# VectorE's order in the front of a conditioned residual kernel: products taken out of their bank first in a period, sums and rotary factors last

## The chip, the core and the metric

The kernel is written for Trainium2 and runs on one core of one chip. A core has TensorE (PE: matmuls, and its weight loads, PEld), VectorE (DVE), ScalarE (ACT), GpSimd (POOL) and SyncE (SP), which here only issues DMAs. Each engine works off its own list of instructions in order and waits on semaphores for the others. TensorE writes its results into PSUM[...]; VectorE and ScalarE read them from there.

The metric is the device time of one execution in microseconds (us), the median over several runs.

## The reference

`x` has 64 batches of 32 rows and 512 columns, in float32. Four layers are added to it one after the other:

```python
x = x + _L0_cond_ref(x, itok_B_0_15, L0_cond_weights)        # x mixed over its 32 rows by one of 16 matrices
x = x + _L1_cond_ref(x, itok_B_6_15, base_weight, base_bias, lora_A_w, lora_B_w)
x = x + _L2_cond_ref(x, Wq, Wk, Wv, Wo, q_norm_w, k_norm_w, k_cache, v_cache, table, seqlens)
x = x + _L3_cond_ref(x, L3_cond_weights, itok_B_0_15)        # mixed over its rows again
```

- Layers 0 and 3: `einsum('bct,bcd->bdt', x, W)`, with the 32 x 32 matrix `W = weights[condition]`.
- Layer 1: `x @ base_weight.T + base_bias`, plus a LoRA term of rank 16, `(x @ A.T) @ B.T`, whose A and B are picked for each batch out of 32 adapters.
- Layer 2: attention. q (32 heads of 128), k and v (8 heads of 128) are projections of x. q and k are normalised by their root mean square, weighted and turned by rotary angles of the position. Keys and values are 512 cached rows (16 pages of 32 rows, picked by a table, masked by the cache's length) and the 32 new ones. Softmax, the weighted sum of values, and an output projection `Wo` from 4096 to 512 columns follow.

## The kernel before

**Tiling.** The 64 x 32 rows of x are 16 tiles `t` of 128 rows (4 batches each). The 8 heads of k and v are two groups `g` of 4 (`KG`), with 16 heads of q each. A `Unit` is one batch in one group, 128 of them; it takes 4 periods, one for each head of k.

**Periods.** All of layers 0 to 2 is one list of numbered periods. The function `slot(i)` (L1193) writes out the instructions of period `i`, which fixes each engine's order. What has to happen in which period is entered beforehand by `at(slot, where, do, ...)` into lists by name ("pe", "late", "power", "turn", "dve", "keep", "act", "store", ...), and `run(slot, where)` (L940) emits one list in the order in which its entries were made. The whole runs under a manual schedule, so nothing is moved afterwards. Periods from 0 on hold the attention: scores of one head, softmax, transposes of its result two periods later, and products with the values three periods later.

**The front.** Periods -43 to -1 come before the first scores. In them run

- layers 0 and 1, class `First`, one tile in two periods. In the even period TensorE multiplies by LoRA's A (`h_ps`, L474), by three of four parts of the base weight (`l_ps`, L490), mixes the next tile (`mix_ps`, L435) and transposes an earlier result (`x2T_ps`, L452); VectorE masks the ranks (`hT`, L484) and adds the mix to x (L444). In the odd period TensorE does the rest of `l_ps` and transposes the next tile (`x1T_ps`); VectorE adds the product to x (L444) and lays out a later tile's mixing matrix (`mix_diag`, L426). GpSimd adds the bias (L447) and issues the gathers;
- the transposes of 16 blocks of cached keys, class `Turn` (`page_rows`, L272), which SyncE loads (L256) and stores again (`kT`, L293; values L289). There are 5 buffers for the loaded rows, so a load waits for the store of the block five before it;
- the rotary factors of all 16 tiles, `rotary` (L382): four VectorE instructions for a tile, or eight or twelve in a period, whose results SyncE stores (L397);
- the projections of the first pair of tiles.

**Projections.** Two tiles form a pair, and for k and v together and for each two heads of q a `Block` computes them with seven products in place of eight. It needs sums of blocks of weights (`block_sum`, L615, one instruction of 128 x 1024) and of the transposed x (`First.sums`, L516 to L520, four instructions), both made by VectorE. Each product is two chunks of two matmuls (`project`, L651), in one or two periods as the table in the plan has it. A product's PSUM tile is `proj_ps`, in a pool with one buffer; some products between periods -11 and -3 lie in `s_ps` instead. `take` reads a finished product out and adds it to what it belongs to (`raw`, L663): on ScalarE for the first product of a block, on VectorE for the six others (two instructions for the sixth). The next product can't begin in the bank before. Afterwards a head's squares go to ScalarE (L707), the power to GpSimd (L714), and four pieces (scale L719, straight L726, swapped L738, sum L748) to VectorE, which `norm_piece` (L950) deals out, up to three in a period; then TensorE transposes the heads (`head_ps`, L756).

**VectorE's order in a period.** "late" and "power" hold the work of layers 0 and 1, then comes one piece of a norm, and after it the list "dve", then two more pieces. The list "dve" was begun when the plan was set up: the rotary factors, the weights' sums and the sums of x are in it from then on. The takes are put into it by `begin_block` (L973), when a block begins, and so stand behind these.

**Into the attention.** In period -7 SyncE loads the next pair's `x_12` over the one that TensorE reads last in that period; in period -6 it issues the 16 page loads of the first unit's keys (`kT`, L794), which the first scores wait for.

**After the attention** the output projection (`out_ps`, L1320) and layer 3 (`mix_ps`, L1338) run, from about 2096 us on.

Of the kernel before, what the change touches and what calls it, by code (L numbers as in the profile page):

```python
# [77 lines left out]
def resid_kernel(  # L78
# [149 lines left out]
    with ExitStack() as l2:  # L228
# [708 lines left out]
        def at(slot, where, do, *args):  # L937
            plan.setdefault((slot, where), []).append((do, args))

        def run(slot, where):  # L940
            for do, args in plan.pop((slot, where), ()):
                do(*args)
# [7 lines left out]
        def norm_piece(slot):  # L950


            if not pieces or pieces[0][0] > slot or busy.get(slot, 0) >= 2 + (slot % 4 == 1):
                return
            busy[slot] = busy.get(slot, 0) + 1
            _, piece, norm = pieces.pop(0)
            piece()
            if norm:
                slot += 1
                while slot in turning or (slot - VLAG) % KG == KG - 1:  # L960
                    slot += 1
                turning.add(slot)
                at(slot, "turn", norm.turn)
                at(slot, "keep", norm.keep)
# [8 lines left out]
        def begin_block(pair, b, slots):  # L973
            block = Block(pair, b, slots)
            for i in range(7):
                for c in (0, 1):
                    at(slots[2 * i + c], "pe", block.project, i, c)
                last = slots[2 * i + 1]
                norm = None
                if i in (1, 4, 5, 6):  # L980
                    if b != KV:
                        norm = Norm(pair, i // 5, 2 * b + (i in (4, 5)))
                    else:
                        norm = Norm(pair, i // 5)
                    if b == KV and i in (1, 6):
                        at(last, "store", block.store_values, norm, i // 5)
                    else:
                        at(last, "pe", begin_norm, last, norm)
                at(last, "act" if i == 0 else "dve", block.take, i, norm)
                busy[last] = busy.get(last, 0) + (0, 1, 1, 1, 1, 2, 1)[i]  # L990

        def call(table, key, name, *args):
# [9 lines left out]
        for i in range(n_pairs):  # L1002
# [14 lines left out]
            for b, slots in (  # L1017
                (KV, (0, 0, 1, 2, 3, 3, 4, 5, 6, 6, 7, 8, 9, 9)),
                (0, (10, 11, 12, 12, 13, 14, 15, 15, 16, 17, 18, 18, 19, 20)),
                (1, (21, 21, 22, 23, 24, 24, 25, 26, 27, 27, 28, 29, 30, 30)),  # L1020
            ):
                slots = [home + w for w in slots]
                at(slots[0], "fetch", begin_block, i, b, slots)
# [169 lines left out]
        def slot(i):  # L1193
            run(i, "fetch")
            run(i, "pool")
            new, k = None, i % KG
            if 0 <= i < n:
                new = unit_of[i // KG]
                new.scores(k)
            if LAG <= i < n + LAG:  # L1200
                turned = unit_of[(i - LAG) // KG]
                turned.flip((i - LAG) % KG)
            run(i, "pe")
            run(i, "late")
            run(i, "power")
            norm_piece(i)
            if LAG <= i < n + LAG and (i - LAG) % KG == KG - 1:
                turned.flip_new()
            run(i, "turn")
            if i >= VLAG:  # L1210
                old = unit_of[(i - VLAG) // KG]
                old.values((i - VLAG) % KG)
                if (i - VLAG) % KG == KG - 1:
                    old.values_new()
                    at(i, "act", old.finish)
                    if old.j == NB - 1:
                        at(i + 1, "store", old.store)
            if new:
                new.divide(k)
            run(i, "dve")  # L1220
            norm_piece(i)
            norm_piece(i)
            run(i, "keep")
            run(i, "act")
            run(i, "store")
# [270 lines left out]
```

## Time and profile before

| | |
|---|---|
| Runs | 2500.81, 2500.87, 2497.43 us; median 2500.81 |
| Profiled execution | 2498.24 us; span from first to last instruction 2496.5 us |
| Busy over the span | PE 98%, PEld 74%, DVE 64%, ACT 56%, POOL 47% |
| Mean granted clock of TensorE | 0.997 |
| First product of the projections (period -33) | 43.3 us |
| First scores (period 0) | 218.5 us |
| First product of the output projection after the attention | 2112.4 us |

How to read the views: the stages' view gives for each stretch the busy time of each engine, the granted clock of TensorE as a share of full speed, and DMA. The view of waits names who waited for whom, with the total, the number of waits and the longest. The timeline lists instructions by start and duration; in brackets at the end stands the idle time of the engine before it, with the releaser that the profile infers from semaphores. "issue" there means that it shows none. Instructions overlap in the engine's pipeline, so the distance from start to start is shorter than the duration. In the DVE timeline the line L663 is `take`, L615 a weight sum, L382 rotary factors, L516 to L520 sums of x, L444 an addition to x.

### The profile page before, as it was taken

What the parts mean: (1) busy time and instruction counts of PE and PEld (TensorE: products, weight loads), DVE (VectorE), ACT (ScalarE), POOL (GpSimd) and SP (SyncE); (2) the same over time, 40 slices, a digit from 0 to 9 for tenths busy, and PEclk for the clock granted to TensorE, in tenths of its full rate; (3) what the DMA queues carried; (4) which work ended last, traced back from release to release, by engine and by line L of the source; (5) the groups of instructions that cost most, each with busy time, mean ns of one, the idle gap of its engine ahead of it and who ended that gap; (6) DMA issues with size and microseconds to landing.
All of it is one profiled execution on the core that took longest, in us unless ns stands there. A gap on an engine that the chain in (4) does not pass through costs nothing.

```text
span 2496.5 us, 47363 instructions
## 1 busy us (share of the span) xinstructions
PE 2445.1 (98%) x13760; PEld 1857.8 (74%) x13760; DVE 1609.0 (64%) x3602; ACT 1398.9 (56%) x4135; POOL 1163.0 (47%) x1096
## 2 busy tenths in 40 slices
PE   7799999999999999999999999999999999999999
PEld 4455777777777777777777777777777788888887
DVE  5657777767777677777776777777777766433222
ACT  2225777777767676767777777777777765000000
POOL 4335655555555555655555555655555663000000
PEclk9999999999999999999999999999999999999999
DMA  7775666666666667766565656666657784333221
GB/s 244 237 218 182 190 196 192 203 184 201 184 201 185 200 193 239 242 188 194 178 199 173 188 176 189 176 186 176 193 169 220 247 267 149 115 128 127 86 85 60
DMA packets 448546, 459.19 MB, mean 184 GB/s; under 512 B 51425, under 2 KB 379489, under 8 KB 440481
## 3 DMA queue, kind: packets, MB, share of 16 engines
q1 hardware_dynamic: 398384, 291.24, 38.0%
q0 software_dynamic: 49904, 164.93, 21.6%
q8 instruction: 112, 1.84, 0.3%
q14 instruction: 146, 1.19, 0.2%
HBM read 384.66 MB, written 79.69 MB: 186 GB/s over the span
## 4 chain that ended last, share of the span: by engine, by line
PE 92%; DMA 2%; DVE 2%; issue 2%; SPq 1%; POOL 1%; ACT 0%; DVEq 0%; POOLq 0%; ACTq 0%
PE proj_ps L651 22%; PE o_ps L893 17%; PE out_ps L1320 15%; PE s_ps L838 10%; PE s_ps L841 8%; PE pT_ps L880 8%; PE head_ps L756 3%; PE l_ps L490 2%; PE o_ps L905 2%; DMA kT<-kT 1%; DMA v_sb<-v,v_rows 1%; SPq L794 1%; PE s_ps L873 1%; PE h_ps L474 1%; PE mix_ps L1338 1%
## 5 line engine op out<-in xcount | busy, mean ns | idle before, releaser
L105 POOL DMA_INDIRECT v_sb<-v,v_rows x512 | 539.2, 1053 | 362.3 <-PE o_ps L893 252.9
L846 DVE CUSTOM_DVE_ANT_0 sm<-s_ps,pen 128x544 f32<-128x544 f32 x512 | 370.9, 724 | 462.4 <-PE s_ps L841 449.9
L893 PEld LDWEIGHTS o_ps<-pT,v_sb 128*128 128x128 f32 x4096 | 518.8, 192 | 133.6 <-issue 124.8
L857 ACT ACTIVATE sm<-sm,top 128x544 f32<-128x544 f32 x512 | 382.0, 746 | 342.8 <-DVE top L846 342.7
L893 PE MATMUL o_ps<-pT,v_sb 128*128 128x128 f32 x4096 | 541.2, 275 | 2.4 <-DMA v_sb<-v,v_rows 2.4
L863 ACT ACTIVATE sm<-sm,share 128x512 f32<-128x512 f32 x512 | 369.9, 722 | 170.3 <-DVE share L862 169.0
L882 DVE COPY pT<-pT_ps 128x512 f32<-128x512 f32 x512 | 351.1, 686 | 1.9 <-PE pT_ps L880 1.9
L838 PE MATMUL s_ps<-kT,qT 128*128 128x288 f32 x1024 | 347.0, 420 | 4.5 <-DMA kT<-kT 3.8
L880 PE MATMUL pT_ps<-ident,sm 128*128 128x128 f32 x2048 | 307.3, 273 | 0.0
L841 PE MATMUL s_ps<-kT,qT 128*128 128x256 f32 x1024 | 305.0, 380 | 1.9 <-issue 1.5
L880 PEld LDWEIGHTS pT_ps<-ident,sm 128*128 128x128 f32 x2048 | 255.8, 141 | 51.3
L809 POOL TENSOR_SCALAR pen<-key_f,seq_f 128x544 f32<-128x544 f32 x128 | 279.3, 2182 | 11.8 <-DMA kT<-kT 0.5
L712 POOL TENSOR_SCALAR ss<-ss 128x4 f32<-128x4 f32 x160 | 54.1, 338 | 448.0 <-ACT sq L707 447.6
L841 PEld LDWEIGHTS s_ps<-kT,qT 128*128 128x128 f32 x1024 | 194.2, 190 | 56.9 <-issue 3.4
L663 DVE TENSOR_TENSOR raw<-proj_ps,raw 128x512 f32<-128x512 f32 x332 | 223.5, 685 | 9.7 <-PE proj_ps L651 4.4
L707 ACT ACTIVATE sq<-raw 128x128 f32<-128x128 f32 x640 | 197.1, 308 | 29.7 <-DVE raw L663 14.5
L651 PE MATMUL proj_ps<-sum,x 128*128 128x512 f32 x380 | 189.7, 602 | 8.0 <-DVE raw L663 7.9
L1370 ACT COPY p<-out_ps 128x256 f32<-128x256 f32 x7 | 2.6, 372 | 333.1 <-PE out_ps L1320 333.1
L714 POOL TENSOR_TENSOR rstd<-ss,minus_half 128x4 f32<-128x4 f32 x160 | 183.0, 1144 | 13.3
L105 POOL DMA_INDIRECT mix_rows<-in_w,cond_rows x32 | 32.7, 1021 | 309.8 <-DVE mix_diag L171 300.0
L838 PEld LDWEIGHTS s_ps<-kT,qT 128*128 128x128 f32 x1024 | 154.7, 191 | 21.9 <-issue 4.8
L1320 PE MATMUL out_ps<-w,o_in 128*128 128x256 f32 x768 | 167.1, 379 | 0.0
(175 smaller groups left out, 3499.4 us busy)
## 6 DMA issues: line engine op xcount, KB each, us to landing
kT<-kT SPq DMA_DIRECT2D x2048, 64.0 KB
o<-oT SPq DMA_DIRECT2D x29, 1024.0 KB
o_in<-o SPq DMA_DIRECT2D x28, 1024.0 KB
page_rows<-in_kv_cache SPq DMA_DIRECT2D x32, 256.0 KB
v<-in_kv_cache SPq DMA_DIRECT2D x32, 256.0 KB
kT<-page_rows SPq DMA_DIRECT2D x32, 256.0 KB
vn<-raw SPq DMA_DIRECT2D x32, 256.0 KB
v_sb<-v,v_rows POOLq DMA_INDIRECT x512
```

The costliest lines, as they stand in the source:

```text
L105: nc.gpsimd.indirect_dma_start(out=dst, out_offset=None, in_=table, in_offset=bass.IndirectOffsetOnAxis(ap=index, axis=0),)
L651: nc.tensor.matmul(self.ps, lhsT=self.pair.x[x][:, c if x == "b" else half.start + c, :], rhs=blocks(self.b)[w][:, c, :], start=(c == 0), ...
L809: nc.gpsimd.tensor_scalar(self.pen, key_f, seq_f[:, self.b : self.b + 1], BIG, ALU.is_ge, ALU.mult)
L838: nc.tensor.matmul(ps[:, first:HID], lhsT=q, rhs=self.kT[:, :n1, k, :], start=True, stop=True)
L841: nc.tensor.matmul(ps[:, HID : first + LA], lhsT=q, rhs=self.kT[:, n1:, k, :], start=True, stop=True)
L846: nc.vector.tensor_tensor_reduce(out=sm, in0=ps[:, first : first + LA], in1=self.pen, scale=1.0, scalar=3e38, op0=ALU.add, op1=ALU.min, ac ...
L857: nc.scalar.activation(sm, sm, AF.Exp, bias=top, scale=-1.0, accum_out=total)
L863: nc.scalar.activation(sm[:, :L], sm[:, :L], AF.Copy, scale=share)
L880: nc.tensor.transpose(ps[:, c, :], self.sm[k][:, c * P : (c + 1) * P], ident)
L882: nc.vector.tensor_copy(pT, ps)
L893: nc.tensor.matmul(self.o_ps[k], lhsT=self.v[c][:, k * D : (k + 1) * D], rhs=self.pT[k][:, c, :], start=(c == 0), stop=False,)
L1320: nc.tensor.matmul(ps[:, :HALF], lhsT=o[:, i, :], rhs=w[i // REP][:, i % REP, :], start=(i == 0), stop=(i == KG * REP - 1),)
```

## The change

In the front (periods below 0) VectorE's takes get a list of their own, "take", which `slot` runs directly behind the list "pe", ahead of layers 0 and 1's work of the period. What is left in the list "dve" there, the sums of weights and of x and the rotary factors, is run at the end of VectorE's work in the period, behind all three pieces of norms. From period 0 on nothing is changed: the takes are in "dve" and it is run where it was.

```diff
@@ begin_block
                     else:
                         at(last, "pe", begin_norm, last, norm)
-                at(last, "act" if i == 0 else "dve", block.take, i, norm)
+                at(last, "act" if i == 0 else "take" if last < 0 else "dve", block.take, i, norm)
                 busy[last] = busy.get(last, 0) + (0, 1, 1, 1, 1, 2, 1)[i]
@@ slot
             run(i, "pe")
+            run(i, "take")
             run(i, "late")
             run(i, "power")
             norm_piece(i)
...
             if new:
                 new.divide(k)
-            run(i, "dve")
+            if i >= 0:
+                run(i, "dve")
             norm_piece(i)
             norm_piece(i)
+            run(i, "dve")
             run(i, "keep")
             run(i, "act")
             run(i, "store")
```

## The prediction

> **What bounds the kernel now.** I read TensorE's busy time by stage first. Columns: stretch, length, busy us (and count) of PE, PEld, DVE, ACT, POOL, granted TensorE clock, DMA share, GB/s.
>
> ```profile
> 0.00:43.30 43.30, 30.02 (x107) 17.77 (x108) 20.30 (x39) 8.37 (x13) 20.28 (x33) 1.00 0.80 261
> 43.30:205.50 162.20, 140.62 (x525) 77.45 (x524) 96.92 (x218) 41.05 (x110) 53.76 (x53) 0.95 0.67 213
> 205.50:231.10 25.60, 20.31 (x82) 11.65 (x80) 21.23 (x47) 16.90 (x50) 18.12 (x19) 1.00 0.69 203
> 231.10:2096.00 1864.90, 1858.42 (x11207) 1408.50 (x11208) 1333.96 (x3108) 1321.09 (x3935) 1054.37 (x970) 1.00 0.66 198
> 2096.00:2496.50 400.50, 395.70 (x1848) 342.40 (x1846) 136.54 (x193) 11.48 (x30) 16.44 (x22) 1.00 0.27 99
> ```
>
> From 231 us on TensorE idles 11.3 us in 2265. The front from the first product (43.3, period -33) to the end of period -7 (205.5) idles 21.6 us of 162.2, at clock 0.95. DMA share 0.67 and DVE 60% say that neither is full there. The waits of PE in that stretch name the releaser (total, times, longest):
>
> ```profile
> PE proj_ps L651 <- DVE raw L663: 15.3, 8, 4.1
> PE proj_ps L651 <- issue: 5.1, 1, 5.1
> PE proj_ps L651 <- ACT raw L671: 1.2, 1, 1.2
> ```
>
> So it is the products' single bank (`proj_ps`): the next product waits until `take` has read the last. The timeline around the longest wait, PE then DVE, shows that the 5.1 filed under "issue" is the same thing:
>
> ```profile
> 87.47 1.02 PE L651 MATMUL proj_ps<-wk,x 128*128 128x512 f32 x2
> 88.33 0.60 PE L452 MATMUL x1T_ps<-ident,x_sb 128*128 128x128 f32 x4
> 94.00 3.65 PE L651 MATMUL proj_ps<-sum,x_b 128*128 128x512 f32 x4 [5.08 <-issue]
> ```
> ```profile
> 86.12 1.22 DVE L615 TENSOR_TENSOR sum<-wq,wq 128x1024 f32<-128x1024 f32 x1
> ...
> 88.87 0.69 DVE L444 TENSOR_TENSOR x_sb<-l_ps,x_sb 128x512 f32<-128x512 f32 x1
> 89.47 0.96 DVE L426 TENSOR_TENSOR mix_diag<-mix_rows,same 128x128 f32<-128x128 f32 x1
> 90.35 0.41 DVE L516 TENSOR_TENSOR x<-x_b 128x256 f32<-128x256 f32 x1
> ...
> 92.62 1.28 DVE L663 TENSOR_TENSOR raw<-proj_ps,raw 128x512 f32<-128x512 f32 x2
> 98.58 0.29 DVE L484 TENSOR_TENSOR hT<-h_ps,lora_mask 128x128 f32<-128x128 f32 x1 [4.68 <-PE h_ps L474]
> ```
>
> The product is complete at 88.3, yet VectorE does a weight sum, 8 factors, the addition, sums of x and 4 factors before the takes at 92.62; then it idles 4.68 us. Work is in the wrong order, not too much of it. And the product after the wait runs 3.65 us instead of 1.88.
>
> [...]waits of 2.77, 3.16, 4.09 and 5.08 us were followed by half rate, 2.39 us (at 218.47) was not. [...]the takes start only after all that stands ahead. [...]here mix_diag took 0.96 us at 89.47, against 0.29 elsewhere, beside GpSimd's bias addition at 89.02. I keep 1 us a tile for it.
>
> **The change, part by part.** No instruction is added or removed: 3361 rows on VectorE in both; TensorE, ScalarE, GpSimd and SyncE keep their order. Only VectorE's order in periods below 0 changes.
>
> (a) Takes go first. What it can free: 15.3 + 5.1 = 20.4 us of waits, plus the half clock: 3.65, 3.63 and 3.62 against 1.88 at 94.00, 138.50 and 175.78 (5.3 us), and at 122.97 until the next mix product 6.98 against 4.33 us in the undisturbed period at 107.92 (2.65 us). Together 7.9, so at most 28.3 us. The 1.2 us behind ScalarE's take stay.
>
> (b) Sums and factors go last, so they now stand ahead of the *next* period's take. I laid both orders side by side at the issue intervals of the DVE timeline: take and addition 0.60, weight sum 1.13, factor 0.20, four sums of x 1.46, swapped 0.67, scale or rotary sum 0.60, hT and diag 0.20. In an even period the tail starts when the mix product ends: 0.1 + addition 0.6 + sums and factors. TensorE meanwhile does x2T 0.44, the rest of l_ps 1.72, its product 0.86 or 1.72, transposes 0.44 each. The worst is -26 to -25: tail 0.7 + 1.13 + 8 x 0.20 = 3.44 us; two takes end at 4.64; TensorE wants the bank at 0.44 + 1.72 + 0.86 + 0.44 = 3.46. **Wait 1.2 us** where it was 5.08. For -28 the tail is 2.96 against 3.88 at which the product ends; for -22, 3.5 against 4.3; for -20, 2.6 against 3.5; behind the double take of -15 TensorE waits 0.1. After odd periods the take has slack: the longest tail (12 factors in -27) ends 3.8 us after its product, and hT, queued behind it, is needed at 7.8. So 1.3 us stay[...].
>
> (c) Behind a take that waits for its product stand the addition, diag and hT. The addition is wanted by x2T one period later, behind product, h_ps, l_ps and mix (0.86 + 0.89 + 2.58 + 0.87 = 5.2 us); it comes at most 1.5 us later. Nothing.
>
> (d) Behind the factors stand SyncE's stores of them (28 `rot` stores), and behind these the loads of x and pages. They come up to 2 us later in the period. Page loads run 17.6 us (154.01 to the transpose at 171.6) or more ahead of use; that lead hides it. Without it each would cost its 2 us.
>
> (e) After period -7 the chain is SyncE's, not VectorE's: the load of x_12 waits for TensorE's last read, then 16 page DMAs are issued.
>
> ```profile
> 205.55 0.32 SPq L586 DMA_DIRECT2D x<-xS  x1
> 206.74 10.04 SPq L794 DMA_DIRECT2D kT<-kT  x16
> ```
>
> The first scores start at 218.47, 13 us after 205.5. The take wait of 1.67 us at 213.66 shrinks to about 0.6 and becomes wait for kT: 2.39 grows to about 3.5 us, gain nothing, and the clock now halves there. Price: between 0 (hidden behind the v_sb wait that ends at 231.04) and 1.8 us; I take 0.7.
>
> Sum: 28.3 - 1.3 - 1.3 - 0.7 = 25.0 us. The profiled execution took 2498.24 us (span 2496.5 and 1.7 around it), 2.6 below the median of 2500.81. Profile after: about 2473; median: **2475.5 us** (-1.0%). From 231 us on all moves earlier unchanged: VectorE's order for periods 0 and up is the same.
>
> **Rivals.**
> R1, the page loop becomes the bound: in the front each page's load waits for the store of the page five before. 149.58 (store) to 154.01 (load) is 4.4 us, the loop 6.0 us (147.99 to 154.01). Periods -23 to -12 cost TensorE 70.1 us, less 10.2 waits and 4.4 half clock: 55.5 / 11 = 5.05 us each. So SyncE falls behind 0.95 us a period. Against it: lead 17.6, less 3 periods x 1.3, less 5 x 0.95, leaves about 9 us where a load needs some 4.4. For it: the same bytes in 16% less time, share 0.67 to 0.79. If landing grows to 7 us, five loops lose 2.6 us each, 13 us in all: 2489.
>
> R2, the waits only move to the tails: each even tail 1.5 us longer than laid out[...] returns about 1.5 to 3 us in four or five periods and, past 2.8 us, the half clock: 10 us lost, 2486.
>
> R3, slower: R1 with the loop at full price. Each us of landing costs 5 us over five loops once the lead is gone; the gain of 25 is eaten and the end passes 2501 only when landing exceeds about 10.5 us against 4.4, so 2508 at 12. Only DMA engines full for long could do that; 343 and more GB/s was moved around 15 us at share 0.93, the front needs 255.
>
> R4, no effect: excluded by order unless DVE's order weren't what holds the bank; the timeline says it is. 2500.
>
> **How the numbers follow.** Main case 0.70 (own range 2469 to 2482: the ceiling of 28.3 us taken from the fastest run, 2497.43, up to 6 us less gain than forecast); R1 0.11, R2 0.12, R3 0.04, R4 0.03. The range 2469 to 2488 holds the main case, R2 and part of R1. Faster than 0.2% (below 2495.8, about what a measurement can tell from no change): 0.70 + 0.12 + 0.10 = 0.92; same 0.04; slower 0.04.
>
> **What would show it.** Right: the waits of `proj_ps` for `raw` between the first product and the first scores fall from 20.4 us to under 4, no piece of that stretch but the first scores at half clock, the stage of 162.2 us near 137, kT's wait before the first scores longer than 2.39. Wrong: PE waiting for page_rows or x_sb from DMA (R1), DVE idle in L382 on DMA stores of `rot` and new waits of 2 to 3 us at takes of odd periods (R2), or a changed length of the stretch after the first scores.

## The result, and the profile after

| | before | after |
|---|---|---|
| Runs, us | 2497.43 to 2501.68, median 2500.84 (4) | 2471.99 to 2476.62, median 2472.82 (4) |
| Ratio after / before | | 0.9893, 95% interval 0.9876 to 0.9911 |
| Span of the profiled execution | 2496.5 us | 2471.8 us |
| First product / first scores | 43.27 / 218.47 us | 44.22 / 191.17 us |

The kernel is 28.0 us faster by the medians (1.1%), 24.7 us by the two profiled spans. The forecast was 25.3 us by the median (2500.81 to 2475.5), 2.7 us less than measured; its range held the result.

The first view is again TensorE's busy time by stage, of the kernel after, cut at the same events (start, first product, end of the last product of period -7, the wait of the first products with the values, `o_ps`); the last cut lies 1864.9 us behind that in both kernels. Columns: stretch, length, busy us (and count) of PE, PEld, DVE, ACT, POOL, granted TensorE clock, DMA share, GB/s.

```profile
0.00:44.20 44.20, 30.61 (x106) 17.95 (x107) 20.26 (x39) 8.34 (x13) 20.32 (x33) 1.00 0.77 255
44.20:178.30 134.10, 131.39 (x524) 74.18 (x523) 94.97 (x216) 40.60 (x110) 57.15 (x53) 1.00 0.79 258
178.30:205.10 26.80, 21.02 (x82) 11.48 (x80) 22.25 (x48) 17.37 (x50) 18.75 (x20) 1.00 0.68 198
205.10:2070.00 1864.90, 1858.28 (x11198) 1408.40 (x11199) 1333.43 (x3105) 1319.51 (x3932) 1061.48 (x969) 1.00 0.66 197
2070.00:2471.80 401.80, 396.98 (x1856) 343.37 (x1854) 138.33 (x196) 12.45 (x32) 16.50 (x22) 1.00 0.27 99
```

The second row is the whole gain: 162.2 us became 134.1, with the same 524 or so matmuls. Two things went out of it. The idle time fell from 21.6 us (162.2 less 140.6) to 2.7 (134.1 less 131.4), and the busy time itself fell by 9.2 us at a clock of 1.00 in place of 0.95. The other rows take 3.4 us of those 28.1 back: 0.9 ahead of the first product, where the change does nothing, 1.2 in the third row, and 1.3 behind it. The table puts these 1.3 us into its last row only because the fourth was cut at equal length; they lie in the attention, which takes 1882.6 us from that `o_ps` product (205.06) to the first product of the output projection, and took 1881.4 before. From there to the end both take 384.1 us. From that `o_ps` product to the end of the span it is 2265.5 us before and 2266.7 after; other traces told below, with the same order there, have 2266.0 (the changed kernel again, third chip), 2268.3 (loads of pages one period later) and 2271.0 (the shorter dummies).

The view of waits of TensorE from the first product to 232 us, after. Columns: what waited for what, total us, times, longest.

```profile
PE proj_ps L651 <- DVE raw L663: 1.8, 2, 1.6
PE proj_ps L651 <- issue: 1.3, 1, 1.3
PE o_ps L893 <- issue: 1.3, 1, 1.3
PE s_ps L838 <- DMA kT<-kT: 1.3, 1, 1.3
PE proj_ps L651 <- ACT raw L671: 1.2, 1, 1.2
PE s_ps L838 <- issue: 0.7, 1, 0.7
PE head_ps L756 <- DVE rot_a L748: 0.5, 1, 0.5
```

The three rows of `proj_ps` together are 4.3 us; up to the end of period -7 its waits were 21.6 us and are 2.7 now (1.3, 1.2 and 0.2). The longest one left there is the double take that used to cost 5.08 us. TensorE and VectorE in the timeline around it, after (start, duration, engine, line; the idle time ahead in brackets):

```profile
84.53 1.02 PE L651 MATMUL proj_ps<-wk,x 128*128 128x512 f32 x2
85.39 0.60 PE L452 MATMUL x1T_ps<-ident,x_sb 128*128 128x128 f32 x4
87.32 1.95 PE L651 MATMUL proj_ps<-sum,x_b 128*128 128x512 f32 x4 [1.33 <-issue]
```
```profile
83.19 1.22 DVE L615 TENSOR_TENSOR sum<-wq,wq 128x1024 f32<-128x1024 f32 x1
84.32 0.29 DVE L382 TENSOR_TENSOR rot<-trig,q_cos 128x128 f32<-128x128 f32 x1
...
85.93 1.28 DVE L663 TENSOR_TENSOR raw<-proj_ps,raw 128x512 f32<-128x512 f32 x2
87.13 0.68 DVE L444 TENSOR_TENSOR x_sb<-l_ps,x_sb 128x512 f32<-128x512 f32 x1
87.73 0.28 DVE L426 TENSOR_TENSOR mix_diag<-mix_rows,same 128x128 f32<-128x128 f32 x1
87.93 0.42 DVE L516 TENSOR_TENSOR x<-x_b 128x256 f32<-128x256 f32 x1
```

The weight sum and eight factors of period -26 still stand ahead of the takes, and they begin where they did: 1.34 us before the product (83.19 and 84.53; before, 86.12 and 87.47). What went from between them and the takes is the addition, the mixing matrix, the four sums of x and four factors, which took from 88.87 to 92.62 before, 3.75 us. That is the whole difference of the two waits, 5.08 and 1.33 us. The product behind the wait takes 1.95 us where it took 3.65 at a granted clock of 0.53 (before, 94.00 to 97.65).

What follows period -7 did not go as the prediction had it. TensorE there, after, those lines with a wait:

```profile
183.21 0.63 PE L756 MATMUL head_ps<-ident,rot_a 128*128 128x128 f32 x4 [0.48 <-DVE rot_a L748]
...
187.18 1.98 PE L651 MATMUL proj_ps<-wv,x_a 128*128 128x512 f32 x4 [1.62 <-DVE raw L663]
...
191.17 0.72 PE L838 MATMUL s_ps<-kT,qT 128*128 128x288 f32 x2 [1.27 <-DMA kT<-kT]
...
205.06 0.49 PE L893 MATMUL o_ps<-pT,v_sb 128*128 128x128 f32 x2 [1.29 <-issue]
```

The wait at the take of period -3 is 1.62 us (1.67 before), and that for the keys became shorter, 1.27 for 2.39. VectorE shows why the first did not shrink (timeline, after):

```profile
178.46 0.69 DVE L663 TENSOR_TENSOR raw<-s_ps,raw 128x512 f32<-128x512 f32 x1 [2.48 <-PE s_ps L651]
179.06 0.68 DVE L444 TENSOR_TENSOR x_sb<-l_ps,x_sb 128x512 f32<-128x512 f32 x1
179.66 0.68 DVE L719 TENSOR_TENSOR raw<-raw,rstd 128x512 f32<-128x512 f32 x1
...
186.44 0.69 DVE L663 TENSOR_TENSOR raw<-proj_ps,raw 128x512 f32<-128x512 f32 x1
```

The take of period -7, now first in its period, waits 2.48 us for its own product, and an addition and a scale, which ran ahead of it before (204.77 and 205.38), wait behind it. From 178.46 to 187.04 VectorE then works with no pause over 0.1 us: takes, pieces of norms and the last four sums of x. The take at 186.44 is late because of that run of work and not because of the order inside its period. SyncE's chain kept its length: the load of `x_12` and 16 page loads begin at 178.45, right behind the product of -7, and the first scores come 12.7 us later, as before (205.55 to 218.47 is 12.9).

### The profile page after: what moved, and what is told of

Read it like the earlier page. It is cut to its first block, busy times and chain, and to the rows that moved or that the text cites. A ratio compares the mean times of both kernels' runs of the same rounds, so it can differ in the third digit from the quotient of the medians.

```text
span 2471.8 us, 47357 instructions
## 1 busy us (share of the span) xinstructions
PE 2438.3 (99%) x13760; PEld 1855.4 (75%) x13760; DVE 1609.2 (65%) x3602; ACT 1398.3 (57%) x4135; POOL 1174.2 (48%) x1096
## 4 chain that ended last, share of the span: by engine, by line
PE 95%; DMA 2%; issue 2%; SPq 1%; DVE 0%; POOL 0%; ACT 0%; DVEq 0%; POOLq 0%; ACTq 0%
PE proj_ps L651 23%; PE o_ps L893 18%; PE out_ps L1323 15%; PE s_ps L838 11%; PE s_ps L841 9%; PE pT_ps L880 9%; PE l_ps L490 3%; PE head_ps L756 3%; PE o_ps L905 2%; DMA kT<-kT 1%; PE h_ps L474 1%; SPq L794 1%; PE s_ps L873 1%; PE mix_ps L1341 1%; PE mix_ps L435 1%
## 5 line engine op out<-in xcount | busy, mean ns | idle before, releaser
L809 POOL TENSOR_SCALAR pen<-key_f,seq_f 128x544 f32<-128x544 f32 x128 | 285.0, 2227 | 11.6 <-issue 0.3
```

Source lines behind the costliest of these rows:

```text
L809: nc.gpsimd.tensor_scalar(self.pen, key_f, seq_f[:, self.b : self.b + 1], BIG, ALU.is_ge, ALU.mult)
```

## The experiments

The kernel before had a median of 2497.92 us on the chip of the first four runs told here, 2498.98 us on a second (the long dummies, the two single runs on pages and the last experiment) and 2499.74 us on a third, where it is named. Times are medians; a result without an interval is one execution. The first product comes at 42.0 to 44.2 us in these traces, ahead of all that is changed, so times in different traces are compared counted from it.

### Each half of the change alone

The prediction gives all of the gain to the takes' place (step a) and none to moving the rest behind the norms. The two halves, each from the kernel before. Takes first, the rest where it was:

```diff
-                at(last, "act" if i == 0 else "dve", block.take, i, norm)
+                at(last, "act" if i == 0 else "take" if last < 0 else "dve", block.take, i, norm)
...
             run(i, "pe")
+            run(i, "take")
             run(i, "late")
```

> Half of the change alone: VectorE's takes directly behind the products, sums and factors left where they were, ahead of the last two norm pieces. My theory (the gain is the takes' place; where sums and factors stand among norm pieces of the same period is nearly free, since both lie ahead of the next period's take): 2472 to 2476 us, one wait of about 1.3 us for the bank left at the double take's product, no half clock in the stretch of the projections. Rival (the end of the period for sums and factors carries part of the gain): 2480 us or more, with waits of the products for takes of over 5 us in sum.

Measured: 2471.5 us (2469.75 to 2474.55), ratio 0.9896, interval 0.988 to 0.9913. Waits of TensorE, first product to 240 us, in this kernel:

```profile
PE s_ps L838 <- DMA kT<-kT: 2.0, 1, 2.0
PE proj_ps L651 <- DVE raw L663: 1.8, 2, 1.6
PE proj_ps L651 <- issue: 1.3, 1, 1.3
PE proj_ps L651 <- ACT raw L671: 1.2, 1, 1.2
```

And the whole list "dve", takes included, moved behind the norms:

```diff
-            run(i, "dve")
+            if i >= 0:
+                run(i, "dve")
             norm_piece(i)
             norm_piece(i)
+            run(i, "dve")
```

> The other half alone: the whole list with sums, factors and takes (still in that order, takes last) moves behind the last two norm pieces, in the front only. My theory: takes move only in the three periods where a norm piece used to follow them, by 0.6 to 0.7 us each; 2500 to 2503 us, products waiting 20 to 23 us for takes, the four half-clock stretches still there. Rival (this half carries part of the gain): under 2494 us.

Measured: 2499.45 us, ratio 1.0007, interval 0.9998 to 1.0016. Waits in the same stretch:

```profile
PE proj_ps L651 <- DVE raw L663: 18.5, 9, 4.2
PE proj_ps L651 <- issue: 5.1, 1, 5.1
```

The kernel before, there (the row of 5.1 us is the same):

```profile
PE proj_ps L651 <- DVE raw L663: 16.9, 9, 4.1
```

The half rate stood behind three of the four long waits (5.08, 4.20 and 3.46 us; the product behind the last took 3.78 us) and not, as expected, behind all four (3.15 us, last section). What follows: takes first is the whole change. It alone has the whole gain and leaves the same three rows of `proj_ps` as the full change; where sums and factors stand among the norms is worth nothing that these runs can tell.

### How far forward the takes must be

The kernel after, with the takes behind layers 0 and 1's work of the period (additions, diagonals and masks):

```diff
-            run(i, "take")
             run(i, "late")
             run(i, "power")
+            run(i, "take")
```

> The changed kernel with the takes behind the work of layers 0 and 1 (mask of ranks, addition to x, mixing matrix) but still ahead of norm pieces, sums and factors. My theory (the price before was sums and factors ahead of the takes, not these): in even periods the take now waits for the mix product, 4.3 us behind its own, but the next product in that bank starts 2.2 us or more after that, so 2471 to 2476 us and products waiting under 3 us for takes. Rival (being directly behind the product is what counts): about 1 us in each of some ten periods, 2480 to 2486 us.

Measured: 2474.36 us (2470.65 to 2476.68), ratio 0.9902, interval 0.9885 to 0.9918. In its timeline the double take has a wait again that is followed by half rate:

```profile
88.71 3.55 PE L651 MATMUL proj_ps<-sum,x_b 128*128 128x512 f32 x4 [2.80 <-issue]
```

A second one of 1.29 us appears at 113.01. Up to the end of period -7 products wait 4.6 us in all for VectorE's takes where under 3 were expected. The first scores come 151.8 us after the first product (195.57 and 43.76), 3.8 us later than in the kernel with takes first alone (148.0; 191.50 and 43.47), but the medians of 2474.36 and 2471.5 have ranges that overlap. So the trace shows a price of about 4 us for layers 0 and 1's work ahead of the takes, most of it at two products; the times neither confirm nor deny it.

### More work in the tails

Step (b) lays the tail of an even period beside TensorE's work. To test that arithmetic, the tail is made longer: the kernel after, with the rotary factors of all tiles but the first two computed twice (the same values written again; some 11 us of VectorE in all, by 0.20 us for each of 56 factors).

```diff
-            for kind in "qk":
+            for kind in "qk" if t < 2 else "qkqk":
```

> The changed kernel with each tile's rotary factors from the third on computed twice: 56 instructions more, 11.3 us of VectorE at 0.20 each. By the tails worked out in the prediction: the wait of 1.33 us behind the double take grows by 8 x 0.20 to about 2.9 and brings the half clock (1.8 us) with it; all other tails still end in time, up to 0.7 us lost at two more places. So 2475 to 2479 us, some 4 us over the changed kernel, of 11.3 added. Rival (VectorE itself is now the bound of the front): 11 us more, 2484.

Measured: 2479.48 us (2473.26 to 2483.96), ratio 0.9928, interval 0.9905 to 0.9952; profiled span 2475.5. The double take's wait is the one that was worked out, and it brings the half rate back for more than 3 us:

```profile
88.21 3.75 PE L651 MATMUL proj_ps<-sum,x_b 128*128 128x512 f32 x4 [2.94 <-issue]
91.76 1.91 PE L474 MATMUL h_ps<-x1T,aT 128*128 128x128 f32 x8
93.46 3.16 PE L490 MATMUL l_ps<-base_sb,x1T 128*128 128x512 f32 x6
```

The product took 3.75 us for 1.95, the eight matmuls of `h_ps` 1.91 for 1.05. A second wait, of 1.14 us, appears at 113.75. Counted from the first product, the first scores come 6.5 us later than in the trace of after (153.4 for 147.0). So of some 11 us added to VectorE about 6 show, at two products: VectorE as a whole isn't the bound. The expected loss of some 4 us was too small; the half rate lasted longer than the one product for which it was reckoned, and the median lies 8.0 us above that of takes first on the same chip, with runs that spread over 10.7 us. The tail is where a limit comes next when VectorE gets more to do, and the layout of step (b) says in which period first.

### What the half rate costs

7.9 of the forecast's 28.3 us were half clock. To take that away and leave the waits, TensorE gets products of no use to do while it waits: the kernel before, with dummies ahead of the four products that waited longest.

```diff
                 x, half, w = self.ORDER[i]
+                idle = {-24: 8, -20: 6, -18: 3, -12: 4}.get(self.slots[2 * i], 0) if c == 0 else 0
+                if idle:
+                    warm = ps_t.tile([P, HID], F32, name="warm_ps", tag="t")
+                    for _ in range(idle):
+                        nc.tensor.matmul(
+                            warm, lhsT=ident, rhs=lora["base"][:, 0, :], start=True, stop=True
+                        )
```

> The kernel before with matmuls of no use (8, 6, 3 and 4 of 128x512, 0.43 us each, into the head bank) put ahead of the four products that wait longest, at 88.9, 118.9, 135.7 and 172.6 us, so that TensorE idles only 0.7 to 1.7 us at each and not 2.8 to 5.1. My theory (7.9 us of the gain are the half clock that followed the idling, 20.4 us the idling itself): the four products run at 1.88 us each and the time falls by about 7 to 8 us, to 2493, with the takes as late as before. Rival (the half rate has another cause, or the clock counts nothing for the end): 2500 to 2503.

Measured: 2499.67 us, ratio 1.0, interval 0.999 to 1.001. No gain, against the expectation of 7 to 8 us. It doesn't decide, for the dummies were too long: one such product is two records, 0.86 us, so the eight ahead of the product of period -24 took 7.03 us and overran the wait of 5.08. In its trace the four products have no half rate (1.88 us at 94.69), and the first scores come 172.0 us after the first product, 3.2 us earlier than before, which the median doesn't show. With 5, 3, 2 and 2 of them (third chip):

```diff
-                idle = {-24: 8, -20: 6, -18: 3, -12: 4}.get(self.slots[2 * i], 0) if c == 0 else 0
+                idle = {-24: 5, -20: 3, -18: 2, -12: 2}.get(self.slots[2 * i], 0) if c == 0 else 0
```

> The kernel before, with products of no use (two records of 0.43 us each, 0.86 us) ahead of the four products that waited longest: 5, 3, 2 and 2 of them, so 4.3, 2.6, 1.7 and 1.7 us of the waits of 5.08, 4.09, 2.77 and 3.16 us. Their results are not used. Theory: the half rate was 7.9 of the 28.3 us and comes from TensorE's idling, so without it the four products run at 1.88 to 2.0 us, the products begin when their takes are done as before, the first scores come 6 to 8 us earlier and the time falls by 5 to 8 us, less up to 1.8 us if the half rate appears at the first scores instead: 2490 to 2494 us beside 2498. Rival: a product behind a wait is long in the records alone, or the time is taken back at the start of the attention: the time stays within 2 us of the kernel before.

Measured: 2494.83 us (2491.27 to 2496.78, 10 runs), ratio 0.9977, interval 0.9968 to 0.9986. The stages' view of this kernel, from the first product to the first scores and the 21.5 us behind it:

```profile
44.10:211.36 167.26, 152.80 (x580) 82.72 (x578) 107.99 (x240) 49.26 (x141) 61.01 (x64) 1.00 0.69 222
211.36:232.90 21.54, 21.47 (x98) 14.89 (x99) 15.56 (x38) 13.66 (x35) 13.97 (x11) 0.92 0.78 230
```

The stretch to the first scores took 175.2 us before (43.27 to 218.47) and 167.3 here, with the takes as late as ever: 7.9 us, the sum of the prediction. The time fell by 4.9 us by the medians, 3.5 to 8.0 by the interval of the ratio. The half rate now falls on the first scores (second row, 0.92), for which up to 1.8 us was deducted beforehand, but in this trace it costs nothing that lasts: the `o_ps` product that waited for its values before comes 179.9 us after the first product and 187.8 us in the kernel before, 7.9 us again. Why the medians show less than that stays open. (The profiled execution was the longest of the ten: it has one wait of 5.30 us at 2039 us, in the attention, without a releaser in the profile.) So the half rate is a price of its own, paid behind these waits: it went when TensorE was kept at work in them (granted clock 1.00 to the first scores, 0.95 before), and it goes when they are removed (1.00 after).

### The page loop

Rival R1 let the loop of page loads become the bound. The prediction estimated that 9 us of lead would remain; in the kernel after, the last two loads are issued at 144.04 and 151.37 and the transposes that use them begin at 149.60 and 156.96, so 5.6 us remain. Nothing waited for them, but it was nearer than estimated. Two experiments squeeze the loop, both from the kernel after. First, the loads entered one period later:

```diff
-            at(home - 3 if c > 3 else begin, "fetch", make, turn_of, key, Turn, 0, c, start_pool, 5)
+            at(home - 2 if c > 3 else begin, "fetch", make, turn_of, key, Turn, 0, c, start_pool, 5)
```

> The changed kernel with each load of cached keys to be transposed entered one period later, so that in SyncE's queue it no longer stands directly behind the store that it waits for. The trace of the changed kernel shows leads of only 5.6 us between the last two of these loads and their transposes. If the page loop (store, wait for landing, load) is what makes SyncE late, the loads now go without that wait, the leads of the last two are no shorter than 5.6 us, and time is 2471 to 2475. If SyncE isn't made late by it, the leads lose a period of 5 us and TensorE waits some 4 us for each of the last two or three: 2480.

Measured: 2470.54 us, no wait for page rows. Timed on the third chip, beside the changed kernel itself:

> The changed kernel with the loads of cached keys entered one period later, as in the single look, now timed. If the page loop binds nothing after the change (theory), 2470 to 2474 us, no different from the changed kernel on the same chip by more than 2 us; if the loop had come within reach of TensorE (rival), waits for page rows appear and it is 3 to 8 us slower than the changed kernel.

> The changed kernel itself, on the same chip as the two others, to compare with: 2470 to 2476 us.

Measured: 2471.66 us (2468.03 to 2474.18), ratio 0.9881, for the later loads; 2471.39 us (2466.84 to 2474.15), ratio 0.9881, for the changed kernel; both intervals 0.9866 to 0.9896. No difference. What SyncE waited for between 80 and 170 us was another matter. After:

```profile
SPq L256 <- DMA kT<-page_rows: 14.3, 6, 5.5
SPq L397 <- DVE rot L382: 8.6, 13, 2.1
```

With the loads one period later:

```profile
SPq L397 <- DVE rot L382: 11.6, 15, 2.2
...
SPq L256 <- DMA page_rows<-in_kv_cache: 0.3, 1, 0.3
```

The loads that come earlier in SyncE's list wait 14.3 us in all for buffers, and what stands behind them waits too. Entered later they find their buffers free, and the last load is issued at 145.95 in place of 151.98 in the changed kernel's run on that chip, so its lead is longer (10.6 us for 4.5). The loop of 7 to 8 us that stands in the trace of after is thus SyncE's list waiting at loads that came too early, and not a limit of the DMA engines: their share between 80 and 165 us is 0.84 there, and 0.89 in the next experiment, which has them move more (278 GB/s for 271).

Second, more bytes: each block of cached keys of the first group stored once more, into a tensor that nothing reads.

```diff
+    kT_again = dram.tile([PAGES, D, KG * PSIZE], F32, name="kT_again")
...
+                if not self.g:
+                    nc.sync.dma_start(
+                        out=kT_again[4 * c : 4 * c + 4].rearrange("p d f -> d p f"),
+                        in_=self.turned.rearrange("d p k s -> d p (k s)"),
+                    )
```

> The changed kernel with a second store of every transposed block of group 0's keys, into memory that nobody reads: 256 KB and one more DMA to issue a block, and the load five blocks later waits for it too. Rival R1 close to binding (lead 5.6 us at the end, landing 4.4 or more): each of the last five loops grows by some 1.5 us, TensorE waits about 6 us in sum for page rows at the last two or three transposes, 2479. If there is slack as the prediction had it (9 us of lead): no wait for pages, 2472 to 2475.

Measured: 2474.77 us. The lead of the last load fell to 3.6 us (155.80 to 159.44) at a DMA share of 0.89 between 80 and 165 us (0.84 after), and still TensorE waited for no page. It waited for a take instead. VectorE in this kernel, and the product behind the take:

```profile
117.80 1.28 DVE L388 TENSOR_TENSOR rot<-trig,q_cos 128x128 f32<-128x128 f32 x1 [2.68 <-DMA rot<-rot]
...
119.62 0.68 DVE L669 TENSOR_TENSOR raw<-proj_ps,raw 128x512 f32<-128x512 f32 x1
```
```profile
120.35 1.98 PE L657 MATMUL proj_ps<-sum,x 128*128 128x512 f32 x4 [2.32 <-DVE raw L669]
```

The expectation of waits for pages was wrong. Of the two ways in which DMA can reach the front, the one that gave first is the second rival's: a rotary factor in the tail waits for the store of an older one, and the take stands behind it. (That factor then takes 1.28 us, the three behind it 0.28 each.) In the kernel after the same waits exist (at 90.06 and 123.43, 0.58 and 1.60 us), but there is slack for them.

### What now sets the start of the attention

If VectorE's run of work from 178.46 on is what holds the take of period -3, moving work out of it should bring the attention forward. From the kernel after: the last four sums of x two periods later, the entry into the attention begun two periods earlier (`ready`), and the weight sum of period -26 one period later.

```diff
-                    (7, 0, 2),
+                    (8, 0, 2),
...
-        ready = -6
+        ready = -8
...
-                at(home + 4, "dve", call, *f, "sums")
-                at(home + 5, "store", call, *f, "store_sums")
+                late = 2 * (t == NT - 1)
+                at(home + 4 + late, "dve", call, *f, "sums")
+                at(home + 5 + late, "store", call, *f, "store_sums")
```

> The changed kernel with three more moves: the weight sum of period -26 goes to -25 (out of the tail ahead of the double take), the first units' key pages are issued two periods earlier, ahead of the load of x_12 that waits for TensorE, and the last four sums of x go two periods later (out of the tail ahead of the last takes). My theory: 0.5 of the 1.33 us, the wait of 1.27 us for the keys and most of the 1.62 us at the last take go, a wait of some 1.3 us for the first values stays: 2 to 3 us less, 2470, near what a measurement tells. Rival: the first values (gathers behind the masks on GpSimd) set the start of the attention and take over what is freed: within 1 us of the changed kernel.

Measured: 2476.71 us (2474.27 to 2476.89), ratio 0.9902, interval 0.9885 to 0.9919: no gain over the change. What was to go did in part: the take of period -3 has a wait of 0.78 us for 1.62, that for the keys is gone, and that behind the double take is 1.14 us for 1.33. The first unit's first scores come 145.9 us after the first product (188.77 and 42.84), 1.0 us earlier than in the trace of after, but its second head's are held up. TensorE and VectorE in this kernel, and GpSimd's mask:

```profile
195.50 1.33 PE L838 MATMUL s_ps<-kT,qT 128*128 128x288 f32 x2 [4.28 <-DVE top L846]
```
```profile
194.71 0.73 DVE L846 CUSTOM_DVE_ANT_0 sm<-s_ps,pen 128x544 f32<-128x544 f32 x1 [4.55 <-POOL pen L809]
```
```profile
192.56 2.12 POOL L809 TENSOR_SCALAR pen<-key_f,seq_f 128x544 f32<-128x544 f32 x1 [3.31 <-issue]
```

Neither the keys nor VectorE ends last there, but the mask `pen` that GpSimd makes for the first softmax. The timeline files the 3.31 us ahead of it under "issue", but the view of the line that stores the sums of x (L537) names who waited for these stores:

```profile
L537 POOL DMA_DIRECT2D xS<-x x4: 539/548/627, 172.5 to 188.7; - x4
...
who waited for it (us, times):
...
  POOL pen L809: 3.3, 1
```

So the edit made this wait itself: with the last sums of x it moved their stores, which GpSimd issues right ahead of the mask, at 188.08 here and at 185.99 in the trace of after, 3.5 us later counted from the first product. In the text of the kernel the mask's pool is opened where the pool that holds these sums is closed, so the mask may lie in their memory; that was not tried. By that same `o_ps` product this kernel is 3.0 us behind after (163.9 us from the first product for 160.8). It therefore tells nothing of what sets the start of the attention once VectorE's run of work is shortened. In the trace of after VectorE waits 2.48 us for the same mask, which begins there at 191.45, directly behind GpSimd's powers of the norms, so GpSimd is close; an edit that moves the sums and leaves their stores ahead of the mask was not made.

## Why the prediction was right

**What bounded it, and step (a): right, in mechanism and size.** The waits of `proj_ps` to the end of period -7 fell from 21.6 to 2.7 us. Takes first alone gives all of it; the rest alone gives nothing. The half rate, over a quarter of the sum, is confirmed by the useless products: 7.9 us from first product to first scores. That it comes "past 2.8 us" of waiting, as the second rival has it, was an estimate from the trace before, where it stood behind a wait of 2.77 us (138.50: 3.63 us for the product, granted clock 0.54) and not behind one of 2.39; the runs do not show a fixed length (last section). The prediction counted 3361 instructions on VectorE; the traces of both kernels have 3602, and that they are as many in both is what its argument needs.

**Step (b): right.** The double take was to leave a wait of 1.2 us and left 1.33; the period of -15 was to leave 0.1 and left 0.16, as much as before. With the factors doubled, the wait of 2.94 us is where the layout puts it. The second 1.3 us in the prediction's sum, the author's allowance for longer instructions on VectorE and for factors still being stored, were not needed in this stage, which became 28.1 us shorter where 28.3 - 1.3 - 1.3 = 25.7 was forecast. Of the 2.4 us more, 1.1 are waits (18.9 us less, 17.8 forecast) and 1.3 busy time (9.2 us less, where the half rate was put at 7.9). Longer instructions beside GpSimd's are there: after, `mix_diag` takes 1.06, 1.13 and 1.14 us at 57.79, 77.53 and 118.61 and 0.54 to 0.71 at three other places, against 0.28 or 0.29 elsewhere. Each of these six begins during one of GpSimd's bias additions (L447) and ends 0.14 or 0.15 us behind it; together they take 3.5 us more than six of the short ones. What makes them longer there, the traces don't show. The prediction's text keeps 1 us a tile for this and its sum 1.3 us in all, with the factors' buffers. Because the takes stand ahead of it in these periods, the time it loses falls into slack.

**Step (c): right by its result.** Additions behind the takes hold up nothing: in the kernel after TensorE has no wait at `x2T_ps`. Additions, masks and mixing matrices ahead of the takes cost some 4 us in the trace.

**Step (d): right in its result, wrong in its margin.** No load was late for its use. But "leaves about 9 us" was 5.6, since the loop took 7.8 and 7.3 us in place of the estimated 6.0, which was the shortest of the last four spacings of these loads before (7.0, 6.4, 6.0 and 7.1). The term that failed is the loop's constant length: SyncE's loads came so early in the list that they waited for buffers, and each such wait held what stood behind. The later entry shows that the loop itself can go faster.

**Step (e): wrong in both waits, of little weight.** The take's wait was to shrink from 1.67 to 0.6 us and stayed at 1.62; the wait for the keys was to grow from 2.39 to 3.5 us and fell to 1.27, with no half rate, so the 0.7 us for it was not paid. The longer wait for the keys was among the signs that the prediction had named for itself; it did not come. What failed is the assumption that the take of -3 is late by its place in the period. It is late by the whole run of VectorE's work that starts with the take of -7, which now waits for its own product; with four instructions fewer in that run (last experiment, beside two other moves) the wait fell to 0.78 us. Step (e)'s frame held: SyncE's chain from the product of -7 to the first scores kept its 12.7 to 12.9 us, so the length of that stretch hardly moved. In its place came 1.2 us more in the third row of the stages, of which 0.6 is the `o_ps` wait (1.29 for 0.68); the rest isn't traced.

**The sum.** 28.1 us in the stage, less 0.9 ahead of it, 1.2 in the third row and 1.3 in the attention, is the 24.7 us of the two spans, 25.0 in the forecast. That agreement is partly luck: the stage gave 2.4 us more than forecast and the rest 2.7 less. The 0.9 and the 1.3 us lie where the order is the same in both kernels, and no more than traces of one order differ by there: the changed kernel's second trace has its first product at 43.72 and its span at 2470.4 us. The medians' difference of 28.0 us is 3.3 more than the spans' 24.7 because the profiled execution before lies 2.6 us under its median and the one after 0.7 over it. On the third chip the medians differ by 28.4 us. Runs of one kernel lie up to 12 us apart, and no more is read into it.

**The rivals.** R1 and R4 fall: TensorE waited for no page, and the gain came. R2 did not happen, though it is what happens next when a tail grows by some 1.5 us (double factors) or a factor waits 2.7 us for its store (double stores). R3 needed a landing of 10.5 us; after, the six loads that wait for a store are issued 4.0 to 6.4 us behind it. (The two sums don't agree: R1 counts its loss from a landing of 4.4 us, R3 from about 5.4.)

## What to carry to other kernels

When the tile for a result has one buffer and its producer is the bound, the instruction that empties it belongs first in the order of the engine that does so; the rest of that engine's period can stand anywhere that it has slack, and moving it was worth nothing by itself here. To price such a move, lay the emptying engine's queue beside the producer's from the last event that ties them (here the mix product), period by period; count the half rate that the trace shows behind waits of the producer as a loss beside them (here 3.62 to 3.65 us for a product of 1.88, behind waits of 2.77, 3.16 and 5.08 us). Ahead of the next step, look for the loads that wait in their queue for a buffer: entering them later can make them earlier (here the last at 145.95 us in place of 151.98), though it bought no time. And when work is moved later, look for what its stores will now hold up.

## What the runs showed of the hardware

- Half rate behind a wait isn't a matter of that wait's length alone. TensorE's waits of 3.16 us (before, at 175.78: 3.62 us for a product of 1.88, granted clock 0.53) and 2.80 us (takes behind the additions: 3.55 us) were followed by it, the wait of 3.15 us at the same product with "dve" last was not (1.99 us at 176.98), nor that of 2.39 us before the first scores of before; one of 2.06 us before the first scores with the dummies was (1.30 us for two matmuls that take 0.72 in the kernel before). What else decides was not tried.
- A product of 128x128 by 128x512 in float32 is two records of 0.43 us each. Ten records in a row took 4.46 us (shorter dummies, at 89.57).
